# Three edits to a stack of four graph layers: ordered waits on GpSimd, a 128-row tile for the exponentials, and a PSUM tile of its own for the last block product

## The chip, the cores and the metric

The kernel runs on one core of one Trainium2 chip. The metric is the device time of one execution in microseconds (us); a figure for a kernel is the median of several executions. Engines: PE is TensorE's matmul, PEld its weight load, DVE is VectorE, ACT is ScalarE, POOL is GpSimd, SP is SyncE, which here issues all DMAs.

## What is computed

128 graphs of 128 nodes with 512 features go through four layers; each layer ends in a residual sum and a layernorm. Everything is fp32.

```python
def _L0_gnn_ref(X, A, kernel, bias):
    Ah = A + jnp.eye(A.shape[-1], dtype=A.dtype)[None, :, :]
    dh = jax.lax.rsqrt(jnp.sum(Ah, axis=-1))
    An = dh[:, :, None] * Ah * dh[:, None, :]
    return jax.nn.relu(jnp.einsum('bnm,bmf,fc->bnc', An, X, kernel) + bias)

def _L1_gnn_ref(x, adj_matrix, W_qk, W_v):
    q, k = jnp.split(jnp.einsum('bnd,ed->bne', x, W_qk), 2, axis=-1)
    v = jnp.einsum('bnd,ed->bne', x, W_v)
    scores = jnp.einsum('bnd,bmd->bnm', q, k) / ATT_DIM ** 0.5
    w = jax.nn.softmax(jnp.sum(scores * adj_matrix, axis=-1, keepdims=True), axis=1)
    return w * v

def _L2_gnn_ref(x, adj, W):
    deg = jnp.sum(adj, axis=-1, keepdims=True)
    agg = jnp.einsum('bij,bjf->bif', adj, x) / jnp.maximum(deg, EPS)
    return jax.nn.relu(jnp.einsum('bnf,of->bno', jnp.concatenate([x, agg], axis=2), W))

def _L3_gnn_ref(X, A, W, b):
    A_hat = A + jnp.eye(A.shape[-1], dtype=A.dtype)
    d = A_hat.sum(axis=-1) ** (-0.5)
    return jnp.einsum('bij,bjf->bif', A_hat * d[:, :, None] * d[:, None, :], X @ W + b)

x = _layernorm(x + _L0_gnn_ref(x, adj, L0_gnn_kernel, L0_gnn_bias), axis=-1)
x = _layernorm(x + _L1_gnn_ref(x, adj, L1_gnn_W_qk, L1_gnn_W_v), axis=-1)
x = _layernorm(x + _L2_gnn_ref(x, adj, L2_gnn_W), axis=-1)
x = _layernorm(x + _L3_gnn_ref(x, adj, L3_gnn_W, L3_gnn_b), axis=-1)
```

## The kernel before

**Tiles and loop.** Four graphs make a tile, so there are 32 tiles (t). The main loop runs one pass a tile: it does layers 0 and 1 of tile t interleaved with layers 2 and 3 of tile u = t - 1, and prepares tile t + 1. Tiles 0 and 1 are started in `begin` (here called the head), and the last tile is finished after the loop (the tail), where the graphs go in pairs.

**Names.** `ana` holds the adjacency of a tile, scaled by degrees (`d`, `dm`); `anT` and `arT` are its transposes. `agg0`, `agg2`, `agg3` are aggregated features, copied by ACT from the PSUM tiles `p_agg`; `xT1`, `xT2` are transposed x. In the loop x is transposed through DRAM (SP writes `xT2s`, reads `xT2y`, and DVE finishes in 32x32 blocks); at the head and the tail by TensorE (`p_xT`).

**Products with weights.** `project` computes each 128x512 by 512x512 product by Strassen's scheme in Winograd's form, in seven block products B11, T1, B21, B22, T2, T3, T4. `left_sums` makes the sums of the left operand on POOL (s1, s2, s4, and one in place; in the profile `agg3s`, `xT1s` and so on, and the tile's own name for the one in place). The products go to PSUM tiles `p_o` of a pool of five; DVE adds them up in the SBUF blocks `sa`, `sb`, `u2`, `u5` (`s_o`, `sb_o`, `u_o` in the profile) and into x. T2, T3 and T4 share one PSUM tile v: T3 and T4 are accumulated on what is there, so T4 may not start before DVE has read v for the block u5. T4 and what follows it are put off (`tails`) until after the first product of the next projection, except after the last one. Layer 1 does the same with tiles `p_v`.

**Layernorm.** `norm_stats`: DVE's bn_stats and bn_aggr give `mv`; POOL makes `rstd` (an add, then a power) and `mr`; ACT makes `nmr` and applies both to x. For layer 3 `norm_last` takes the sums on ACT (`row`, `square`), and POOL works on `last`.

**Softmax of layer 1.** `l1_scores` has TensorE's `p_sc` and four DVE operations `scr` that leave the row weights `w` (128x4). `l1_softmax` transposes w (`p_w`, 4x128), takes the minimum, the exponential and its sum on ACT, and scales by the reciprocal on DVE: the tile `e` of 4 rows by 128. `l1_add` transposes e back (`p_ws`, 128x4), copies it to `ws`, and adds ws * v to x by four DVE operations for each pair of graphs.

**What sets the order.** All operations are first recorded in a `Plan` with estimated durations. `schedule` is a list scheduler: it simulates the five engines, takes at each step the ready operation with the earliest latest start, and so fixes the order on every engine. It has one resource besides the engines: `port`, that any POOL operation and any DVE operation with two SBUF operands of full size hold while they run, one at a time. `emit` issues the operations in that order. On the chip each engine runs its own queue in order, and waits between engines are made from data dependences alone: the turns at the port are planned, but nothing enforces them. All operations are issued from line 271, so that the profile tells them apart by tile names.

Of the kernel before, what the change touches and what calls it, by code (L numbers as in the profile page):

```python
# [10 lines left out]
FP = mybir.dt.float32  # L11
AF = mybir.ActivationFunctionType
ALU = mybir.AluOpType
AX = mybir.AxisListType

P = 128
K = 32
Q = P // K
G = 4
# [101 lines left out]
class Op:  # L121
    def __init__(self, engine):
        self.engine, self.dur, self.lat, self.size, self.port, self.calls, self.preds, self.succs = engine, 0, 0, 0, False, [], set(), []
        self.last, self.start, self.end = float("inf"), None, None


class Plan:
# [2 lines left out]

    ENGINES = ("tensor", "vector", "scalar", "gpsimd", "sync")
    HOP = 200
    LAND, FLIGHT = 1600, 9
    HEAD, BUS = 40000, (62, 95)

    def __init__(self, nc, est):
        self.nc, self.est, self.ops, self.tags, self.group, self.dram = nc, est, [], {}, None, None
        for e in self.ENGINES:  # L140
            setattr(self, e, Recorder(self, e))

# [54 lines left out]
    def schedule(self):  # L197
        number = {op: i for i, op in enumerate(self.ops)}
        for (_, tag, bufs), tiles in self.tags.items():
            used = []  # L200
            for t in sorted((t for t in tiles if t.ops), key=lambda t: number[t.ops[0]]):
                if len(used) == bufs:
                    old = used.pop(min(range(bufs), key=lambda i: number[used[i].ops[-1]]))
                    assert number[old.ops[-1]] < number[t.ops[0]], (tag, bufs)
                    for op in t.ops:
                        if op.preds.isdisjoint(t.ops):
                            op.preds.update(old.ops)
                used.append(t)
        now = 0
        for op in self.ops:  # L210
            assert all(number[p] < number[op] for p in op.preds)
            for p in op.preds:
                p.succs.append(op)
            if op.engine == "tensor":
                op.last = now
                now += op.dur
        for op in reversed(self.ops):
            due = min([s.last - self.hop(op, s) for s in op.succs], default=now)
            op.last = min(op.last, due - op.dur)
        queue = {e: [] for e in self.ENGINES}  # L220
        waiting = {op: len(op.preds) for op in self.ops}
        free, bus, port = dict.fromkeys(self.ENGINES, 0), 0, 0
        pe = [op for op in self.ops if op.engine == "tensor"]
        for op in self.ops:
            if not op.preds:
                queue[op.engine].append((0, number[op], op))
        done, landed = [], []
        while len(done) < len(self.ops):
            best = None
            for e in self.ENGINES:  # L230
                q = queue[e]
                if e == "tensor":
                    q = [c for c in q if c[2] is pe[0]]
                if not q:
                    continue
                q = [(max(c[0], port if c[2].port else 0),) + c[1:] for c in q]
                at = max(free[e], min(c[0] for c in q))
                pick = min((c for c in q if c[0] <= at), key=lambda c: (c[2].last, c[1]))
                for c in q:
                    if at < c[0] < at + pick[2].dur and c[2].last < at + pick[2].dur and c[2].last < pick[2].last:  # L240
                        pick, at = c, c[0]
                if best is None or at < best[0]:
                    best = at, e, pick[2]
            at, e, op = best
            queue[e] = [c for c in queue[e] if c[2] is not op]
            if e == "sync" and len(landed) >= self.FLIGHT:
                at = max(at, landed[-self.FLIGHT])
            op.start, op.end = at, at + op.dur
            free[e] = op.end
            if op.port:  # L250
                port = op.end
            if e == "sync":
                bus = max(bus, op.end + self.LAND) + op.size / self.BUS[at > self.HEAD]
                op.lat = max(op.lat, bus - op.end)
                landed.append(op.end + op.lat)
            if e == "tensor":
                pe.pop(0)
            done.append(op)
            for s in op.succs:
                waiting[s] -= 1  # L260
                if not waiting[s]:
                    queue[s.engine].append((max(p.end + self.hop(p, s) for p in s.preds), number[s], s))
        return done
# [4 lines left out]
    def emit(self):  # L268
        for op in self.schedule():
            for method, args, kw in op.calls:  # L270
                getattr(getattr(self.nc, op.engine), method)(  # L271
                    *[v.real() if isinstance(v, Ref) else v for v in args],
                    **{k: v.real() if isinstance(v, Ref) else v for k, v in kw.items()})


class Recorder:
# [35 lines left out]
def kernel(  # L312
# [10 lines left out]
    b3: bass.AP,  # L323
    out: bass.AP,
):
    nc = Plan(tc.nc, estimate)
    B = x.shape[0]
    NT = B // G
    last = NT - 1
# [57 lines left out]
        nc.tensor.transpose(p[:, 0], ident, ident)  # L387
    nhalf = const.tile([P, G], FP, tag="nhalf", name="nhalf")
    nc.vector.memset(nhalf, -0.5)
    w0_sb = weight(w0, "w0_sb", nc.sync)  # L390
    b0_sb = broadcast_row(b0, "b0_sb", nc.sync)
    wqk_sb = tp.tile([P, C, 2 * ATT], FP, tag="row", name="wqk_sb", bufs=1)
# [133 lines left out]
    def project(name, t, parts, first, c11, fin, hooks=None, after=lambda: None, pairs=(0, 1), early=True):  # L526

        hooks = hooks or {}  # L530
        qs = slice(pairs[0], pairs[-1] + 1)

        def region():
            return ps_b.tile([P, 2, H], FP, tag="pb", name=f"p_{name}_{t}")[:, qs]

        def operand(left_, k):
            s = st[left_, t]
            if isinstance(s, Ref):
                return s.rearrange("p (q r) (h c) n -> p q r h c n", r=2, h=2)[:, :, 0, (B11, B21).index(k)]
            return s[k]  # L540

        def product(p, k, fresh):
            with nc.unit():
                for q in pairs:
                    for i, (left_, w) in enumerate(parts):
                        for c in range(2):
                            nc.tensor.matmul(p[:, q - pairs[0], :], operand(left_, k)[:, q, c, :], w[:, c, k, :],
                                             start=(fresh and q == pairs[0] and i == 0 and c == 0),
                                             stop=(i == len(parts) - 1 and c == 1), skip_group_check=True)
            for f in hooks.get(k, ()):  # L550
                f()

        def block(tag):
            return tp.tile([P, 2, H], FP, tag=tag, name=f"{tag}_{name}_{t}", bufs=2 if tag == "s" else 1)[:, qs]

        g, q, v = region(), None, None
        product(g, B11, True)
        sa, sb = first(g, block)
        finish_tails()
        if early:  # L560
            product(g, B21, False)
            c11(g, block)
        q = region()
        product(q, T1, True)
        u5 = block("u5")
        nc.vector.tensor_tensor(u5, q, sb, ALU.add)
        if not early:
            product(g, B21, False)
            c11(g, block)
        v = region()  # L570
        product(v, T2, True)
        u2 = block("u2")
        nc.vector.tensor_tensor(u2, v, sb, ALU.add)
        product(q, B22, False)
        nc.vector.tensor_tensor(u2, q, u2, ALU.add)
        fin(0, 1, u2)
        norm_stats(name, t, 0, pairs)
        product(v, T3, False)
        nc.vector.tensor_tensor(u5, v, u5, ALU.add)
        fin(1, 1, u5)  # L580

        def tail():
            product(v, T4, False)
            nc.vector.tensor_tensor(sa, v, sa, ALU.add)
            fin(1, 0, sa)
            norm_stats(name, t, 1, pairs)
            after()

        tails.append(tail)
# [126 lines left out]
    def l1_softmax(t):  # L716
# [1 line left out]
        nc.tensor.transpose(p[:G, :], st.pop(("w", t)), ident)  # L718
        mn = sp.tile([G, 1], FP, tag="mn", name=f"mn_{t}")
        nc.vector.tensor_reduce(mn, p[:G, :], AX.X, ALU.min)  # L720
        e = sp.tile([G, P], FP, tag="e", name=f"e_{t}", bufs=1)
        ssum = sp.tile([G, 1], FP, tag="ssum", name=f"ssum_{t}")
        nc.scalar.activation(e, p[:G, :], AF.Exp, bias=mn, scale=-1.0, accum_out=ssum)
        rsum = sp.tile([G, 1], FP, tag="rsum", name=f"rsum_{t}")
        nc.vector.reciprocal(rsum, ssum)
        nc.vector.tensor_scalar(e, e, rsum, None, ALU.mult)
        st["e", t] = e

    def l1_out(t, hooks):

# [44 lines left out]
    def l1_add(t):  # L775

        p = ps_t.tile([P, P], FP, tag="pt", name=f"p_ws_{t}")
        nc.tensor.transpose(p[:, :G], st.pop(("e", t)), ident[:G, :G])
        ws = sp.tile([P, G], FP, tag="ws", name=f"ws_{t}")
        nc.vector.tensor_copy(ws, p[:, :G])  # L780
        for r in range(2):
# [167 lines left out]
```

## Time and profile before

| what | us |
|---|---|
| median of 3 executions (lowest, highest) | 2450.66 (2450.37, 2451.76) |
| the profiled execution, its own time | 2451.53 |
| its span, first to last instruction | 2449.8 |
| PE busy, 12462 matmuls | 2437.9 |
| DVE busy, 3396 instructions | 1714.5 |
| POOL busy, 1580 instructions | 1316.0 |
| ACT busy, 2117 instructions | 996.4 |
| one pass of the loop (1073.72 to 1149.36) | 75.64 |

The granted TensorE clock is 0.999, and DMAs move 97 GB/s on average. In the profile, a busy time is a sum over instructions, whose ends are modelled for matmuls; in a dense stretch the starts are what to go by. An idle time in brackets is that of the engine just before an instruction, with what released it.

### The profile page before, as it was taken

The numbers are of one execution on the slowest core, as the hardware profiler recorded it, in microseconds if no ns is written. First come the engines' busy times: TensorE is split into PE (matmuls) and PEld (weight loads), VectorE is DVE, ScalarE is ACT, GpSimd is POOL, SyncE is SP. The second block draws the span as 40 slices with busy tenths as digits, with TensorE's granted clock in tenths as the row PEclk, the third lists the DMA queues.
The fourth block names the chain that finished last, engine by engine and source line by source line (L and its number), as shares of the span: only waits on it lengthen the run. The fifth ranks groups of instructions, "written<-read, shape, count | busy, mean of one in ns | idle before, by whom it ended". The sixth has DMA issues, their size and how long they took to land.

```text
span 2449.8 us, 35470 instructions
## 1 busy us (share of the span) xinstructions
PE 2437.9 (100%) x12462; PEld 2087.3 (85%) x12462; DVE 1714.5 (70%) x3396; ACT 996.4 (41%) x2117; POOL 1316.0 (54%) x1580
## 2 busy tenths in 40 slices
PE   9999999999999999999999999999999999999998
PEld 7888888888888888888888888888888888888887
DVE  7767766677666777766776667766677676777666
ACT  4334343443434444344443444333444334443345
POOL 6464555555555555555455554645546455555543
PEclk9999999999999999999999999999999999999999
DMA  5133233442424423244332443234442333423220
GB/s 181 48 99 104 73 108 91 125 125 57 116 78 125 125 69 109 78 121 125 84 93 82 117 125 104 73 99 104 120 125 61 96 102 117 125 74 96 67 80 35
DMA packets 393266, 241.15 MB, mean 98 GB/s; under 512 B 140416, under 2 KB 358016, under 8 KB 393088
## 3 DMA queue, kind: packets, MB, share of 16 engines
q1 hardware_dynamic: 393088, 238.88, 35.4%
q8 instruction: 99, 1.62, 0.3%
q14 instruction: 79, 0.65, 0.1%
HBM read 126.62 MB, written 112.20 MB: 97 GB/s over the span
## 4 chain that ended last, share of the span: by engine, by line
PE 96%; DMA 1%; DVE 1%; POOL 1%; SPq 0%; issue 0%; ACT 0%; POOLq 0%; DVEq 0%
PE p_o L271 61%; PE p_v L271 20%; PE p_agg L271 14%; PE p_sc L271 1%; SPq L271 0%; DMA x<-in_x_dram 0%; PE p_w L271 0%; DVE x L271 0%; DMA xT1s<-x 0%; DVE u_o L271 0%; PE p_ws L271 0%; DMA xT1y<-xT1s 0%; PE p_xT L271 0%; POOL xT2s L271 0%; DMA xT2y<-xT2s 0%
## 5 line engine op out<-in xcount | busy, mean ns | idle before, releaser
L271 PE MATMUL p_o<-w_sb,agg 128*128 128x256 f32 x2048 | 471.3, 380 | 0.9 <-DVE u_o L271 0.9
L271 PEld LDWEIGHTS p_o<-w_sb,agg 128*128 128x128 f32 x2048 | 386.1, 190 | 52.8 <-DVE u_o L271 0.9
L271 ACT COPY agg<-p_agg 128x512 f32<-128x512 f32 (+1 forms) x415 | 226.3, 553 | 406.0 <-PE p_agg L271 405.8
L271 PE MATMUL p_v<-wv_sb,xT 128*128 128x320 f32 x1024 | 291.7, 433 | 0.1
L271 PE MATMUL p_o<-w2x_sb,xT 128*128 128x256 f32 x1024 | 263.0, 379 | 1.0 <-ACT xT L271 1.0
L271 DVE TENSOR_TENSOR v<-p_v,v 128x320 f32<-128x320 f32 x316 | 154.5, 490 | 155.4 <-PE p_v L271 154.8
L271 PE MATMUL p_o<-w2a_sb,agg 128*128 128x256 f32 x1024 | 262.8, 379 | 0.0
L271 PEld LDWEIGHTS p_v<-wv_sb,xT 128*128 128x128 f32 x1024 | 191.9, 190 | 76.7 <-ACT xT L271 0.6
L271 PEld LDWEIGHTS p_agg<-anT,x 128*128 128x128 f32 x2048 | 238.7, 192 | 7.0 <-DVE anT L271 0.5
L271 DVE TENSOR_TENSOR u_o<-p_o,u_o 128x512 f32<-128x512 f32 (+1 forms) x196 | 129.1, 671 | 160.6 <-PE p_o L271 159.1
L271 PE MATMUL p_agg<-anT,x 128*128 128x128 f32 x2048 | 239.4, 275 | 0.3 <-DVE anT L271 0.3
L271 PEld LDWEIGHTS p_o<-w2x_sb,xT 128*128 128x128 f32 x1024 | 194.2, 190 | 30.8 <-ACT xT L271 1.4
L271 PE MATMUL p_v<-wv_sb,xT1s 128*128 128x320 f32 x768 | 217.6, 433 | 0.8 <-POOL xT1s L271 0.6
L271 PEld LDWEIGHTS p_o<-w2a_sb,agg 128*128 128x128 f32 x1024 | 194.6, 190 | 26.4
L271 POOL TENSOR_SCALAR rstdo<-mvo 128x2 f32<-128x2 f32 (+1 forms) x131 | 35.7, 272 | 320.9 <-DVE mvo L271 318.3
L271 PE MATMUL p_o<-w2x_sb,xT2s 128*128 128x256 f32 x768 | 197.2, 379 | 0.0
L271 PE MATMUL p_o<-w2a_sb,agg2s 128*128 128x256 f32 x768 | 197.1, 379 | 0.0
L271 ACT ACTIVATE x<-x,nmro,rstdo 128x512 f32<-128x512 f32 x256 | 195.0, 808 | 3.4
L271 PEld LDWEIGHTS p_v<-wv_sb,xT1s 128*128 128x128 f32 x768 | 145.5, 190 | 59.0 <-POOL xT1s L271 2.0
L271 PE MATMUL p_o<-w_sb,agg0s 128*128 128x256 f32 x768 | 181.1, 379 | 0.4 <-DVE u_o L271 0.4
L271 PE MATMUL p_o<-w_sb,agg3s 128*128 128x256 f32 x744 | 173.8, 383 | 0.0
L271 DVE BATCH_NORM_STATS2 bno<-x 128x6 f32<-128x512 f32 x258 | 170.4, 682 | 3.9
(146 smaller groups left out, 4255.8 us busy)
## 6 DMA issues: line engine op xcount, KB each, us to landing
x<-in_x_dram SPq DMA_DIRECT2D x31, 1024.0 KB, 6.5
out_dram<-x SPq DMA_DIRECT2D x31, 1024.0 KB, 5.4
xT2s<-x SPq DMA_DIRECT2D x120, 256.0 KB, 2.8
xT2y<-xT2s SPq DMA_DIRECT2D x240, 128.0 KB, 2.7
xT1s<-x SPq DMA_DIRECT2D x120, 256.0 KB, 2.5
xT1y<-xT1s SPq DMA_DIRECT2D x240, 128.0 KB, 3.1
sa<-ana SPq DMA_DIRECT2D x120, 128.0 KB, 3.2
ya<-sa SPq DMA_DIRECT2D x120, 128.0 KB, 3.3
```

Of the source, the lines that this page charges most:

```text
L271: getattr(getattr(self.nc, op.engine), method)(*[v.real() if isinstance(v, Ref) else v for v in args], **{k: v.real() if isinstance(v, Ref ...
```

## The change

It has three parts.

- In `schedule`, when an operation takes the port, the plan now also remembers the one that had it before (`owner`). If the new one is on POOL, the former is on DVE, and the POOL operation was otherwise ready less than 500 ns (`CLOSE`) after the port came free, the POOL operation is given a wait on that DVE operation (`op.after`), which `emit` adds. The planned order itself is made as before.
- The exponentials are kept in one constant tile `e_sb` of 128x128, zeroed once at the start; the softmax works on its first 4 rows, as before on the tile e. The transpose back takes the whole tile with the whole identity, so that p_ws is 128x128, of which the first 4 columns are read.
- In the very last projection, DVE adds v to sa before the product T4, T4 goes to a PSUM tile of its own, and sa then takes that.

```diff
@@ class Plan
-    HOP = 200
+    HOP, CLOSE = 200, 500
...
-    def __init__(self, nc, est):
-        self.nc, self.est, self.ops, self.tags, self.group, self.dram = nc, est, [], {}, None, None
+    def __init__(self, tc, est):
+        self.tc, self.nc, self.est, self.ops, self.tags, self.group, self.dram = tc, tc.nc, est, [], {}, None, None
@@ schedule
-        free, bus, port = dict.fromkeys(self.ENGINES, 0), 0, 0
+        free, bus, port, owner = dict.fromkeys(self.ENGINES, 0), 0, 0, None
...
             if op.port:
-                port = op.end
+                ready = max((p.end + self.hop(p, op) for p in op.preds), default=0)
+                if e == "gpsimd" and owner is not None and owner.engine == "vector" and ready < port + self.CLOSE:
+                    op.after = owner
+                port, owner = op.end, op
@@ emit
-                getattr(getattr(self.nc, op.engine), method)(
+                op.ins = getattr(getattr(self.nc, op.engine), method)(
                     *[v.real() if isinstance(v, Ref) else v for v in args],
-                    **{k: v.real() if isinstance(v, Ref) else v for k, v in kw.items()})
+                    **{k: v.real() if isinstance(v, Ref) else v for k, v in kw.items()}).ins
+            if op.after is not None:
+                self.tc.add_manual_dep(op.ins, op.after.ins.name, mybir.DependencyInfo(
+                    mybir.DependencyClass.Sync, mybir.DependencyReason.DATA))
@@ tile_gnn_stack_kernel
+    e_sb = const.tile([P, P], FP, tag="e_sb", name="e_sb")
+    nc.vector.memset(e_sb, 0.0)
@@ project
         def tail():
-            product(v, T4, False)
-            nc.vector.tensor_tensor(sa, v, sa, ALU.add)
+            p = v
+            if (name, t, pairs[-1]) == ("o3", last, 1):
+                nc.vector.tensor_tensor(sa, v, sa, ALU.add)
+                p = region()
+            product(p, T4, p is not v)
+            nc.vector.tensor_tensor(sa, p, sa, ALU.add)
@@ l1_softmax
-        e = sp.tile([G, P], FP, tag="e", name=f"e_{t}", bufs=1)
+        e = e_sb[:G, :]
@@ l1_add
-        nc.tensor.transpose(p[:, :G], st.pop(("e", t)), ident[:G, :G])
+        nc.tensor.transpose(p, e_sb, ident)
```

More of the change, by code (lines that the diff above doesn't have):

```diff
@@ L123, in __init__ @@
         self.engine, self.dur, self.lat, self.size, self.port, self.calls, self.preds, self.succs = engine, 0, 0, 0, False, [], set(), []
-        self.last, self.start, self.end = float("inf"), None, None
+        self.last, self.start, self.end, self.after = float("inf"), None, None, None
 class Plan:
     ENGINES = ("tensor", "vector", "scalar", "gpsimd", "sync")
-    HOP = 200
+    HOP, CLOSE = 200, 500
     LAND, FLIGHT = 1600, 9
     HEAD, BUS = 40000, (62, 95)
-    def __init__(self, nc, est):
-        self.nc, self.est, self.ops, self.tags, self.group, self.dram = nc, est, [], {}, None, None
+    def __init__(self, tc, est):
+        self.tc, self.nc, self.est, self.ops, self.tags, self.group, self.dram = tc, tc.nc, est, [], {}, None, None
         for e in self.ENGINES:
@@ L325 @@
 ):
-    nc = Plan(tc.nc, estimate)
+    nc = Plan(tc, estimate)
     B = x.shape[0]
@@ L726, in l1_softmax @@
         nc.vector.tensor_scalar(e, e, rsum, None, ALU.mult)
-        st["e", t] = e
     def l1_out(t, hooks):
```

## The prediction

> **What bounds the kernel now.** I read the page first, then the waits, then the timeline of one loop pass, of the head and of the tail.
>
> ```profile
> PE 2437.9 (100%) x12462; PEld 2087.3 (85%) x12462; DVE 1714.5 (70%) x3396; ACT 996.4 (41%) x2117; POOL 1316.0 (54%) x1580
> ...
> PE 96%; DMA 1%; DVE 1%; POOL 1%; SPq 0%; issue 0%; ACT 0%; POOLq 0%; DVEq 0%
> ```
>
> TensorE (PE) is the chain and is called busy throughout, so only time inside that "busy" or at the ends can be won. The view of waits shows where weight loads (PEld) came late:
>
> ```profile
> PEld p_ws L271 <- issue: 10.7, 32, 0.4
> PEld p_w L271 <- issue: 9.6, 27, 0.4
> ```
>
> Both are the single small transposes of the softmax, 32 each. The timeline of one pass (start, us):
>
> ```profile
> 1023.57 1.28 POOL L271 TENSOR_TENSOR agg3s<-agg 128x512 f32<-128x512 f32 x1 [8.85 <-ACT agg L271]
> 1023.64 1.76 DVE L271 TENSOR_TENSOR ana<-ana,ident 128x512 f32<-128x512 f32 x1
> 1024.44 1.94 PE L271 MATMUL p_o<-w_sb,agg 128*128 128x256 f32 x8
> 1025.32 0.27 DVE L271 SCALAR_TENSOR_TENSOR scr<-p_sc,dmn,v 128x64 f32<-128x64 f32 x1
> 1026.36 0.27 PE L271 MATMUL p_w<-ident,w 128*4 128x128 f32 x1
> 1026.47 1.89 PE L271 MATMUL p_o<-w_sb,agg3s 128*128 128x256 f32 x8
> 1028.20 1.89 PE L271 MATMUL p_o<-w_sb,agg 128*128 128x256 f32 x8
> 1030.02 0.22 PE L271 MATMUL p_ws<-ident,e 4*128 4x4 f32 x1
> ...
> 1030.17 3.72 PE L271 MATMUL p_o<-w_sb,agg3s 128*128 128x256 f32 x16
> 1033.73 7.07 PE L271 MATMUL p_o<-w_sb,agg 128*128 128x256 f32 x32
> ```
>
> Starts count here, since ends are modelled. Eight p_o take 1.73 (1026.47 to 1028.20). The next eight take 1.82 up to p_ws (0.09 lost), p_ws takes 0.15, and the sixteen behind it 3.56 instead of 3.46 (0.10 lost): one p_ws costs 0.09 + 0.15 + 0.10 = 0.34, in the finer starts 0.348. The same sum holds for all 32 of them, although e was ready between 0.39 and 5.06 us earlier: the loss is not a wait for data.
>
> p_w is different. From 1024.44 to 1026.36 are 1.92; in the pass at 2310.38, where w was ready 0.68 early, the same stretch is 1.78. So 0.145 is lost, in 28 of the 32 passes. There w is late (last scr to p_w 0.155 in each) because scr starts at 1025.32 instead of about 1024.64 (p_sc ends 1024.44, and PE to DVE takes 0.2 in this trace): the ana operation before it took 1.76, beside POOL's agg3s, against 0.68 for the same operation undisturbed (1047.28).
>
> **What the Trainium skill says.** "TensorEngine Tiling (Array Packing)", Key Properties: "Mode switching requires drain". With "TensorE: Matmul & The Clock Gate", step by step: a weight load is pulled ahead of running matmuls if the row groups don't conflict or it goes to the background buffer. The trace agrees for p_ws (4 rows): its load starts at 1030.02 with its own matmul, not before. For 128x128 transposes it finds no loss: eight p_xT from 86.84 to 87.71, 0.109 each, and four p_o behind them at once in 0.87. "SBUF — State Buffer", Who interferes with whom: a DVE instruction with two SBUF inputs and a GpSimd instruction that reads SBUF share a port; whichever is second blocks. The 1.76 against 0.68 agrees.
>
> **The change part by part.** My sum is made against the profiled execution, 2451.53 us (span 2449.8 and 1.7 around it); the median is 2450.66, 0.87 lower.
>
> *Exponentials in 128 rows.* p_ws becomes one 128x128 transpose. I take the 0.109 of p_xT: 0.348 - 0.109 = 0.24 saved, in 31 passes 7.4 us. In the last pass nothing: the PE stall at 2392.00 is set by DVE's chain from p_ws, so an earlier PE waits there longer (0.04 left). Bounds: all of it, 7.7; or none, should the drain belong to the lone transpose rather than its 4 rows. The exponential, reciprocal and multiplication still touch 4 rows. The zeroing at the start lies in DVE's idle time before 3.58. One p_agg a pass gains a wait on a p_ws some 12 us older: nothing.
>
> *GpSimd waits.* The instruction orders are the old ones but for the tail; 347 POOL instructions are given a wait on the DVE operation planned before them. In the trace 287 of these started before that DVE operation ended, so most waits bind. In the loop the first gain is p_w: agg3s has to wait for ana (14 passes ana,ident, 14 ana,d). ana then ends near 1024.33, scr starts on PE's 1024.64, w is ready 0.68 earlier and the 0.145 goes: 28 x 0.145 = 4.1 us. Next late is nothing: in the 2 passes with w early, PE runs on. What stands behind the wait: agg3s starts at about 1024.41 rather than 1023.57, 0.84 later; its result had 1.62 to spare before PE. The other waits of a pass: rstdv on the last x<-v (1.47 later, twice a pass about 1.5 to 1.7) delays nmrv on ACT and the x for PE's p_agg, which had 2.9 or more, and the first transposed-sum xT2s had 1.7 (median). agg3 (T3), up to 3.0 later, had 4.2, and agg2, 2.4 later, 12.5. I cost these at nothing; above, the price is what exceeds the spare.
>
> *Head, to 50 us.* Gain: sb_o (14.58) now follows agg0s, DVE's agg0s are not blocked (2.90 for two before, about 0.8 free), u_o is there at 19 instead of 20.30, and the stall at 20.36 goes: 0.52 + 0.10. Loss: agg0s2 of tile 1 (28.07) waits for DVE's two wv_sb (about 30.5), agg0s4 and agg0 follow x operations, so rstdo behind them runs near 37.1 instead of 34.77, and mro at 38.2 instead of 36.31. ACT's normalisation and copies take 2.4 up to the first p_xT: PE gets it at 40.8 instead of 39.62. Part is recovered, since ACT idled 0.57 and POOL's xT1s was held by rstdo: PE's xT1s product at 47.7 instead of 47.10. Net +0.6; bounds -1.3 (the stalls at 20.36 and from 40.57 to 47.10 are 2.6 in all; half of them gone) and +1.7.
>
> *Tail.*
>
> ```profile
> 2391.77 1.66 DVE L271 SCALAR_TENSOR_TENSOR x<-v,ws,x 128x256 f32<-128x256 f32 x4
> ...
> 2392.46 0.24 POOL L271 TENSOR_TENSOR mrv<-mvv,rstdv 128x2 f32<-128x2 f32 x1
> 2392.73 0.20 ACT L271 ACTIVATE nmrv<-mrv 128x2 f32<-128x2 f32 x1 [7.52 <-POOL mrv L271]
> ...
> 2393.83 2.05 PE L271 MATMUL p_agg<-arT,x 128*128 128x128 f32 x16
> ...
> 2397.43 1.13 PE L271 MATMUL p_o<-w2x_sb,xT 128*128 128x256 f32 x4 [0.68 <-ACT xT L271]
> ```
>
> Here mrv gets a wait on the fourth x<-v, which ends 2393.43: mrv near 2393.5, 1.04 late, and x, p_agg with it, since x was on time by 0.05 alone. At 2397.43 ACT's queue gives 0.4 back (nmrv of the second half no longer holds it). Net +0.65; bounds 0 and +1.1.
>
> *Last block product.*
>
> ```profile
> 2440.41 1.03 PE L271 MATMUL p_o<-w_sb,agg 128*128 128x256 f32 x4
> 2441.47 0.42 DVE L271 TENSOR_TENSOR u_o<-p_o,u_o 128x256 f32<-128x256 f32 x1 [0.44 <-PE p_o L271]
> ...
> 2441.95 1.13 PE L271 MATMUL p_o<-w_sb,agg 128*128 128x256 f32 x4 [0.52 <-DVE u_o L271]
> ...
> 2446.26 0.55 DVE L271 TENSOR_SCALAR x<-x,mvo,rstdo 128x512 f32<-128x512 f32 x1
> ```
>
> T4 in its own PSUM starts at 2441.27 (2440.41 + 4 x 0.216), 0.68 earlier. DVE has one more add (0.42) and becomes the bound: x<-u_o moves into its idle 0.44 before 2441.47, then u_o, the new add, x, the last add at about 2442.5 (before 2443.12), x, two bn_stats, mvo at 2444.25 instead of 2444.57. POOL's order brings rstdo's power straight behind its sum, no longer behind the power of last: end 0.6 earlier. Bounds 0.3 and 0.9.
>
> Sum: -7.4 - 4.1 + 0.6 + 0.65 - 0.6 = -10.9, 2440.6 for an execution like the profiled one, 0.87 less against the median: 2439.7.
>
> **Rivals.** (A) p_w keeps its loss: ana stays slow or scr is held by something else. For: DVE runs other two-input operations there. Against: the two early passes. 2439.7 + 4.1 = 2443.8. (B) The drain stays with p_ws: 2439.7 + 7.4 = 2447.1. For: p_w is a lone transpose with a late load too. Against: p_w with early w (67.10, 98.97) loses nothing. (C) The waits cost 2 to 4 us more in head, tail or some passes: 2442 to 2444. For: queues of POOL and ACT are in order, and the wait's own latency is not in my sums. (D) Slower: the transposed-sum path of a pass. rstdv's wait (1.69 + 0.08) delays x, SP's DMA xT2s (1044.38) behind it, xT2y, the DVE transposes and POOL's xT2s, with 1.72 spare before PE. Reaching PE whole and losing a 0.93 slot of SP's queue, it stalls 2.70 - 1.72 = 0.98 a pass, 29 times 28: 2468. It decides from 2.1 on (1.72 + 10.9/29). Against: nmrv stood behind ACT's row until 1041.90 anyway, so only 0.8 of 1.77 passes.
>
> **How the numbers follow.** Forecast 0.64, A 0.10, B 0.07, C 0.13, D 0.06. The range runs from 2437.2 (head at its good bound) to 2445.5 (C and A in); B and D are outside. 0.2%, 4.9 us, is what a measurement of this kernel can tell from no change: faster is below 2445.8 (forecast, A, C: 0.87), same 0.07 (B), slower 0.06 (D).
>
> **What would show it.** p_ws in a stretch of p_o: 0.11 and no longer load behind it; p_w's lateness gone and ana at 0.68 beside no agg3s; the pass shortened from 75.64 to about 75.25; p_xT near 40.8; p_agg near 1.0 late at the tail. A pass above 75.5, or PE waits in the loop for xT2s, agg3s or x, would prove it wrong.

## The result and the profile after

The changed kernel takes 2439.84 us (median of 5 executions, 2439.40 to 2440.78) where the kernel before takes 2450.66: ratio 0.9953, 95% interval 0.9943 to 0.9964. Its profiled execution took 2440.58 with a span of 2438.8, against 2451.53 and 2449.8 before: 11.0 less span.

The page of the changed kernel, first the busy times, then the chain by engine:

```profile
PE 2425.6 (99%) x12462; PEld 2088.6 (86%) x12462; DVE 1676.0 (69%) x3398; ACT 999.5 (41%) x2117; POOL 1230.8 (50%) x1580
...
PE 95%; DMA 1%; DVE 1%; POOL 1%; SPq 1%; ACT 1%; issue 0%; POOLq 0%; DVEq 0%; ACTq 0%
```

DVE's busy time fell by 38.5 us and POOL's by 85.2, with two DVE instructions more than before. The runs below tell the parts apart: with the added waits alone (e2) the two are busy for 1671.0 and 1233.1, with the 128 rows alone (e1) for 1713.2 and 1317.1. So it is the waits, and part of what had been called busy was one engine held up by the other. Of TensorE's 11.0 only about 4 came from there, and about 7 from the rows of p_ws; the rest of that busy time had not been on its path.

In the view of waits of the weight loads, p_ws and p_w led with 10.7 and 9.6 us. Now the longest are these (us in all, times, longest), and neither p_ws nor p_w is among them:

```profile
PEld p_xT L275 <- ACT xT1y L275: 2.7, 3, 2.0
PEld p_agg L275 <- ACT x L275: 1.3, 1, 1.3
...
PEld p_v L275 <- POOL xT1s L275: 1.3, 2, 0.7
```

The timeline of the pass that the prediction showed (start and duration in us, engine, operation):

```profile
1019.32 0.68 DVE L275 TENSOR_TENSOR ana<-ana,ident 128x512 f32<-128x512 f32 x1
...
1020.12 1.95 PE L275 MATMUL p_o<-w_sb,agg 128*128 128x256 f32 x8
1020.15 1.27 POOL L275 TENSOR_TENSOR agg3s<-agg 128x512 f32<-128x512 f32 x1 [8.30 <-ACT agg L275]
1020.32 0.28 DVE L275 SCALAR_TENSOR_TENSOR scr<-p_sc,dmn,v 128x64 f32<-128x64 f32 x1 [0.31 <-PE p_sc L275]
...
1021.90 0.27 PE L275 MATMUL p_w<-ident,w 128*4 128x128 f32 x1
...
1022.01 1.89 PE L275 MATMUL p_o<-w_sb,agg3s 128*128 128x256 f32 x8
...
1023.74 1.89 PE L275 MATMUL p_o<-w_sb,agg 128*128 128x256 f32 x8
...
1025.25 0.14 PEld L275 LDWEIGHTS p_ws<-ident,e_sb 128*128 128x128 f32 x1
...
1025.46 0.27 PE L275 MATMUL p_ws<-ident,e_sb 128*128 128x128 f32 x1
...
1025.57 3.62 PE L275 MATMUL p_o<-w_sb,agg3s 128*128 128x256 f32 x16
```

ana is done in 0.68 before agg3s starts; scr waits for PE's p_sc and no longer for ana; from 1020.12 to p_w are 1.78, where there were 1.92. Around p_ws nothing is lost: 1.72 for the eight p_o before it (1023.74 to 1025.46), 0.11 for p_ws, whose load now starts 0.21 ahead of it.

The tail, and the end:

```profile
2381.07 1.66 DVE L275 SCALAR_TENSOR_TENSOR x<-v,ws,x 128x256 f32<-128x256 f32 x4
...
2382.87 0.20 POOL L275 TENSOR_TENSOR mrv<-mvv,rstdv 128x2 f32<-128x2 f32 x1 [1.19 <-DVE x L275]
...
2384.20 2.05 PE L275 MATMUL p_agg<-arT,x 128*128 128x128 f32 x16 [0.94 <-ACT x L275]
...
2430.41 1.89 PE L275 MATMUL p_o<-w_sb,agg 128*128 128x256 f32 x8
...
2434.42 0.22 POOL L275 TENSOR_SCALAR rstdo<-mvo 128x1 f32<-128x1 f32 x1
2434.73 0.62 POOL L275 TENSOR_TENSOR rstdo<-rstdo,nhalf 128x1 f32<-128x1 f32 x1
...
2435.38 0.55 DVE L275 TENSOR_SCALAR x<-x,mvo,rstdo 128x512 f32<-128x512 f32 x1 [0.46 <-POOL rstdo L275]
```

mrv now waits 1.19 for the fourth x<-v, and p_agg pays for it. At the end the last eight p_o run as one row, without the 0.68 between the fours.

### The profile page after: what moved, and what is told of

It is laid out like the page before. It is cut to its first block, busy times and chain, and to the rows that moved or that the text cites. A ratio compares the mean times of both kernels' runs of the same rounds, so it can differ in the third digit from the quotient of the medians.

```text
span 2438.8 us, 35587 instructions
## 1 busy us (share of the span) xinstructions
PE 2425.6 (99%) x12462; PEld 2088.6 (86%) x12462; DVE 1676.0 (69%) x3398; ACT 999.5 (41%) x2117; POOL 1230.8 (50%) x1580
## 3 DMA queue, kind: packets, MB, share of 16 engines
q8 instruction: 99, 1.62, 0.3%
## 4 chain that ended last, share of the span: by engine, by line
PE 95%; DMA 1%; DVE 1%; POOL 1%; SPq 1%; ACT 1%; issue 0%; POOLq 0%; DVEq 0%; ACTq 0%
PE p_o L275 60%; PE p_v L275 20%; PE p_agg L275 14%; PE p_sc L275 1%; SPq L275 1%; DMA xT1s<-x 0%; DMA xT1y<-xT1s 0%; POOL xT2s L275 0%; ACT x L275 0%; DMA xT2y<-xT2s 0%; DVE x L275 0%; DVE xT L275 0%; PE p_xT L275 0%; POOL rstdo L275 0%; DVE ana L275 0%
## 5 line engine op out<-in xcount | busy, mean ns | idle before, releaser
L275 ACT ACTIVATE nmro<-mro 128x2 f32<-128x2 f32 (+1 forms) x130 | 26.5, 204 | 368.0 <-POOL mro L275 367.9
```

The costliest lines, as they stand in the source:

```text
L275: op.ins = getattr(getattr(self.nc, op.engine), method)(*[v.real() if isinstance(v, Ref) else v for v in args], **{k: v.real() if isinstan ...
```

## The experiments

All times are medians beside runs of the kernel before on the same chip, whose median there was 2451.86 (e1 to e4), 2451.62 (e5, e6, e7, e9) and 2451.63 (e8, e10 to e12), about 1 us above that of the result. So differences are compared, not times. Where a difference is small, the trace says more than the median. This table is worked out from start times of PE's rows in one trace of each kernel (us, spans to the hundredth, 2449.75 for the kernel before): the head from the first p_agg of tile 0 to the first p_w; the pass as the mean of two passes (p_w of tile 7 to that of tile 9); the passes from the p_w of tile 2 to that of tile 31; the tail from there to the end of the span.

| kernel | head | pass | passes | tail |
|---|---|---|---|---|
| before | 58.79 | 75.633 | 2190.24 | 65.67 |
| after | 59.01 | 75.257 | 2179.93 | 65.38 |
| after, again (e12) | 59.01 | 75.257 | 2179.21 | 65.37 |
| 128 rows alone (e1) | 59.05 | 75.401 | 2183.25 | 65.64 |
| waits alone (e2) | 58.94 | 75.493 | 2185.95 | 66.63 |
| PSUM alone (e3) | 59.31 | 75.632 | 2190.43 | 64.86 |
| 28 waits (e4) | 58.24 | 75.256 | 2180.80 | 64.83 |
| 28 waits, again (e11) | 58.24 | 75.257 | 2178.87 | 64.83 |
| all but the 28 (e5) | 59.00 | 75.401 | 2183.35 | 65.37 |
| 28 and one of the head (e10) | 58.75 | 75.257 | 2179.53 | 64.83 |

### One part at a time

The kernel before with only the tile e_sb and its transpose:

```diff
-        e = sp.tile([G, P], FP, tag="e", name=f"e_{t}", bufs=1)
+        e = e_sb[:G, :]
...
-        nc.tensor.transpose(p[:, :G], st.pop(("e", t)), ident[:G, :G])
+        nc.tensor.transpose(p, e_sb, ident)
```

> The kernel before with only the exponentials in a tile of 128 rows, so that p_ws is one 128x128 transpose. Theory (the 4 rows of p_ws make the array drain): each p_ws then takes 0.11 up to the next matmul, nothing is lost before or behind it, 0.24 is saved in 31 passes, 7.5 us in all: 2443.2. p_w keeps its wait of 0.145. Rival (the loss belongs to a lone transpose, whatever its rows): 2450.7. A second question is the two waits of PE for the transposed-sum product at tile 10 and tile 26, which grew by 0.19 and 0.32 with the whole change: if they grow because PE arrives earlier, they grow here as well; if the added waits make the operands late, they stay at 0.29 and 0.05.

Measured: 2444.88, ratio 0.9971 (0.9959 to 0.9983), 7.0 less. A pass is 0.232 shorter, p_ws takes 0.109 up to the next matmul and 0 is lost before it, and p_w keeps its lateness in 28 passes. The rival falls. On the second question neither reading held: in this execution PE's waits at tile 10 and 26 were gone.

The kernel before with only `op.after` in the plan (the first part of the change's diff):

> The kernel before with only the waits of GpSimd. Theory: -4.1 in the passes (p_w's wait gone), +0.6 head, +0.65 tail: 2447.8. If these waits also make the operands at tile 10 and 26 late, 0.5 more: 2448.3. Rival (p_w late for another reason): nothing won, head and tail lost: 2451.9. Rival (the waits cost in the passes too): above 2449.

Measured: 2448.81, ratio 0.9988 (0.9981 to 0.9995), 3.05 less. A pass is 0.140 shorter and p_w is late nowhere; p_ws still loses its 0.094 before and 0.104 behind. The tail is 0.96 longer: 0.64 of it comes with the late mrv at its start, and 0.3 near its end, where PE waits for the last agg31s; the whole change, whose plan orders this end differently, has no such wait. Both rivals fall.

The kernel before with only the new `tail()`:

> The kernel before with only the last block product in PSUM of its own. Theory: the stall of 0.68 before the last four p_o goes, and PE and DVE end 0.6 earlier: 2450.1, the difference being below what the medians can tell, but not below what the profile of the last 10 us can. Rival (DVE has one more add and is the chain of the end, so that nothing comes of it): p_o starts earlier but the last x and the end do not: 2450.7.

Measured: 2450.87, ratio 0.9996 (0.9988 to 1.0005): not told from no change, as expected. Its trace: the 0.68 before the last p_o is gone, and from the start of the last stretch of p_o<-agg31s (2438.32, before 2437.82) to the end of the span are 11.20 instead of 11.93, and the whole tail is 0.81 shorter, so 0.7 to 0.8 is won and not 0.6. The rival falls.

The three differences, 7.0, 3.05 and 1.0, add up to 11.0, the whole change's 10.8 within what the medians can tell. In the passes the parts don't overlap: 0.232 and 0.140 make 0.372, and the whole change's pass is 0.376 shorter. In the tail they don't simply add (-0.03, +0.96 and -0.81 against -0.29 for the whole), most of the difference being e2's wait for the last agg31s.

### Which of the 347 waits matter

The changed kernel with a wait only where the first agg3s of a pass follows ana (28 waits); `named` gives the name of an operation's output:

```diff
-            if op.after is not None:
+            if op.after is not None and (named(op), named(op.after)) == ("agg3s1", "ana"):
```

> The changed kernel with 28 of its 347 waits: only the first sum of the third layer's aggregates (agg3s, the first of a pass) on the DVE multiplication of the adjacency (ana). Theory (this collision alone made w late): p_w waits for nothing in 28 passes, and head and tail are as before: 2450.7 - 7.5 - 4.1 - 0.6 = 2438.5, about 1.3 below the whole change. Rival (other waits are needed for w, or for order in the passes): p_w keeps 0.145 in some or all passes: 2440 to 2442.6.

Measured: 2439.69, ratio 0.9950 (0.9935 to 0.9964), 12.2 less than before. p_w waits nowhere. The pass is 75.256, the same as with all 347.

The opposite, with `!=` in that line, so that 319 waits stay:

> The changed kernel without those 28 waits of agg3s on ana; its other 319 waits stay. Theory (only these keep ana clear of agg3s): ana takes 1.76 again in these passes and p_w waits 0.145 in 28 of them: 4.1 more than the whole change, 2443.9 where before is 2450.7 (6.7 below before). Rival (the other waits shift GpSimd so far that ana is clear of it anyway, or one wait in an earlier place orders both): p_w waits for nothing, 2439.8 (10.8 below before).

Measured: 2444.17, ratio 0.9970 (0.9957 to 0.9982), 7.45 less than before. p_w is late in 28 passes again and the pass is 75.401, that of e1 to the nanosecond: in the passes the 319 other waits win nothing that PE feels. The timeline of its pass shows the collision again:

```profile
1020.61 1.29 POOL L280 TENSOR_TENSOR agg3s<-agg 128x512 f32<-128x512 f32 x1 [7.46 <-ACT agg L280]
...
1020.69 1.76 DVE L280 TENSOR_TENSOR ana<-ana,ident 128x512 f32<-128x512 f32 x1
...
1022.37 0.27 DVE L280 SCALAR_TENSOR_TENSOR scr<-p_sc,dmn,v 128x64 f32<-128x64 f32 x1
...
1023.41 0.27 PE L280 MATMUL p_w<-ident,w 128*4 128x128 f32 x1
```

agg3s starts 0.08 ahead of ana, and ana ends 0.55 after it. Together e4 and e5 show that for p_w these 28 waits are enough, and needed.

### What makes the small transpose dear

Four forms of p_ws in the changed kernel. The first two are ordinary matmuls of two passes, which differ only in their rows; the plan is told the transpose's duration so that the order stays.

```diff
-        nc.tensor.transpose(p, e_sb, ident)
+        nc.tensor.matmul(p[:, :G], e_sb[:G, :], ident[:G, :G], start=True, stop=True)
```

> The changed kernel with p_ws as an ordinary matmul of the 4 rows of e with a 4x4 identity (two passes, not the transpose's one), as a control for the next run. Theory (4 rows make the array drain before and behind it): in a stretch of p_o about 0.09 lost before its first pass and 0.10 behind its last, as before, with its own time on top.

```diff
+        nc.tensor.matmul(p[:, :G], e_sb, ident[:, :G], start=True, stop=True)
```

> The same matmul with all 128 rows of e and 128x4 of the identity: the same two passes, the same 4 moving columns, only the rows differ from the run before. Theory (rows): nothing lost before it and behind it; p_ws up to the next p_o takes two weight loads of 128 columns at most, about 0.2. Rival (the 4 moving columns make it slow, since too little runs while the next weights load): the same loss as with 4 rows, 0.1 behind it.

```diff
+        nc.tensor.transpose(p[:, :32], e_sb[:32, :], ident[:32, :32])
```

> The changed kernel with p_ws as a transpose of 32 rows with a 32x32 identity. Theory (any tile that doesn't use all rows drains): 0.09 lost before and 0.10 behind it, as with 4 rows. Rival (only a tile of under 32 rows[...] drains): 0.11 and nothing lost, as with 128.

```diff
+        nc.tensor.transpose(p[:, :64], e_sb[:64, :], ident[:64, :64])
```

> The changed kernel with p_ws as a transpose of 64 rows with a 64x64 identity, after 32 rows drained as 4 do. Theory (every tile with fewer rows than the 128 of its neighbours drains): 0.09 lost before it and 0.1 behind it, about 0.37 in all. Rival (half the array is enough to let the load go ahead): 0.11, nothing lost.

One execution each, on two chips, so that the single times alone can't rank the forms. From the last p_o before p_ws to the third behind it, less three undisturbed p_o of 0.216, median of 30 passes:

| rows x moving columns | us | lost before p_ws | single time of the kernel |
|---|---|---|---|
| 4 x 4, transpose (before) | 0.347 | 0.094 | |
| 128 x 128, transpose (after) | 0.111 | 0 | 2440.58 |
| 4 x 4, two passes (e6) | 0.507 | 0.093 | 2452.72 |
| 128 x 4, two passes (e7) | 0.223 | 0 | 2442.97 |
| 32 x 32, transpose (e9) | 0.374 | 0.094 | 2449.02 |
| 64 x 64, transpose (e8) | 0.399 | 0.094 | 2449.34 |

The timeline of one pass of e9 and of e7:

```profile
1027.06 1.89 PE L275 MATMUL p_o<-w_sb,agg 128*128 128x256 f32 x8
1028.88 0.14 PEld L275 LDWEIGHTS p_ws<-ident,e_sb 32*128 32x128 f32 x1 [0.33 <-issue]
1028.88 0.25 PE L275 MATMUL p_ws<-ident,e_sb 32*128 32x32 f32 x1
1029.06 3.72 PE L275 MATMUL p_o<-w_sb,agg3s 128*128 128x256 f32 x16
```

```profile
1024.60 1.89 PE L275 MATMUL p_o<-w_sb,agg 128*128 128x256 f32 x8
1026.11 0.41 PEld L275 LDWEIGHTS p_ws<-ident,e_sb 128*128 128x128 f32 x2
1026.33 0.28 PE L275 MATMUL p_ws<-ident,e_sb 128*128 128x4 f32 x2
1026.47 3.70 PE L275 MATMUL p_o<-w_sb,agg3s 128*128 128x256 f32 x16
```

With 32 rows the eight p_o take 1.82, and the load starts with its own matmul after 0.33 of waiting for nothing that the profile shows. With 128 rows they take 1.73 and the load starts 0.22 ahead, though only 4 columns move. So the loss before p_ws goes with the rows, and half the array is no better than 4 rows: the rivals for e9 and e8, by which 32 or 64 rows pass freely, fall. The rival for e7 is right in part: 4 moving columns lose nothing before, but 0.083 behind, where the second p_o comes 0.299 after the first instead of 0.216. As ordinary matmuls, 128 rows are 0.28 a pass cheaper than 4: 0.09 of it before p_ws, 0.17 from p_ws to the next p_o (0.31 and 0.14), and only 0.02 behind. So that the loss behind p_ws goes with the rows is not shown: with few moving columns most of it stays. That the numbers sit in a constant tile now is not what helps, since e8 and e9 use the same tile.

### Whether the other waits pay, and noise

The changed kernel with the 28 waits and the one at the head that puts sb_o behind DVE's agg0s; the 28 alone again; and the changed kernel as it is:

```diff
-            if op.after is not None:
+            if op.after is not None and (named(op), named(op.after)) in (("agg3s1", "ana"), ("sb", "agg0s4")):
```

> The changed kernel with 29 waits: the 28 of agg3s on ana, and the one of the head that keeps GpSimd's first bias sum off DVE's agg0s. Theory (the other 318 waits win nothing, and those of head and tail cost: at the head p_xT 1.2 later, at the tail p_agg 1.1 later, of which 0.3 and 0.6 reach PE's end): about 1.3 below the whole change, and the stall of 0.5 to 1.0 near 20.4 us gone. Rival (the waits that are left out keep other collisions away that PE does feel): within 0.3 of the whole change or above it.

> The kernel with the 28 waits alone, again, beside the whole change on the same chip. Theory: 0.8 to 1.3 below the whole change, the stall near 20.4 us at the head being there or not from execution to execution. Rival: no difference to the whole change that the intervals can tell.

> The changed kernel unaltered, on the same chip as the two before, as their control: 10.8 below the kernel before.

Measured, five executions each: e10 2439.02 (2438.71 to 2439.25), ratio 0.9948 (0.9935 to 0.9960); e11 2439.48 (2438.89 to 2439.87), ratio 0.9950 (0.9936 to 0.9964); e12 2439.78 (2439.45 to 2439.99), ratio 0.9951 (0.9938 to 0.9963), 11.85 below before. e10 lies 0.76 below the whole change, and no execution of one reaches the other's; at 12.6 below the kernel before it is the furthest of all kernels here, though executions of e11 overlap with it. e11's 0.3 can't be told: that e4 came out about 1.3 further below its kernel before than the whole change had, on another chip, is not confirmed side by side. Both gains are below the expected 1.3 and 0.8: in the tail 0.54 came (65.37 to 64.83), at the head of e10 0.26. There the stall near 20.4 went, but 0.39 appeared before p_o at 35.75.

**Why the head differs between executions of one program.** The timeline of the head of the kernel before, and of the changed one:

```profile
8.72 0.69 DVE L271 TENSOR_REDUCE deg<-ana 128x4 f32<-128x512 f32 x1 [0.47 <-DMA ana<-in_adj_dram]
...
12.33 1.41 DVE L271 TENSOR_TENSOR w_sb<-w_sb 128x512 f32<-128x512 f32 x2
...
19.03 0.67 DVE L271 TENSOR_TENSOR u_o<-p_o,b_sb 128x512 f32<-128x512 f32 x1
```

```profile
9.49 0.69 DVE L275 TENSOR_REDUCE deg<-ana 128x4 f32<-128x512 f32 x1 [1.12 <-DMA ana<-in_adj_dram]
...
13.31 1.41 DVE L275 TENSOR_TENSOR w_sb<-w_sb 128x512 f32<-128x512 f32 x2
...
17.86 0.68 DVE L275 TENSOR_TENSOR u_o<-p_o,b_sb 128x512 f32<-128x512 f32 x1
```

DVE waits for the adjacency of tile 1: 0.47 in before, 0.72 in e1, 0.98 in e3, not at all in e4 and e11. PE's stall near 20.4 was 0.52, 0.77 and 0.97 in the first three and 0.06 at most in the other two: it is that late DMA, handed through. From w_sb to u_o DVE needs 6.70 without waits at the head (before, e3, e4) and 4.55 with them (after, e5): they take 2.15 of blocking out, so that u_o is early and the stall gone although the DMA was 1.12 late. In e10, where sb_o's is the only wait at the head, it is 4.54: that one wait does it.

**Waits in the passes that come and go.** PE's waits for the transposed sum are not the change's either. At tile 10, e4 and e11, which are the same kernel, in two executions:

```profile
774.12 1.30 DVE L280 STREAM_TRANSPOSE xT<-xT1y 128x512 f32<-128x512 f32 x2 [4.13 <-DMA xT1y<-xT1s]
775.57 1.27 POOL L280 TENSOR_TENSOR xT1s<-xT 128x512 f32<-128x512 f32 x1 [4.20 <-DVE xT L280]
776.89 1.10 PEld L280 LDWEIGHTS p_v<-wv_sb,xT1s 128*128 128x128 f32 x5 [1.34 <-POOL xT1s L280]
```

```profile
772.69 1.30 DVE L280 STREAM_TRANSPOSE xT<-xT1y 128x512 f32<-128x512 f32 x2 [2.37 <-DMA xT1y<-xT1s]
774.14 1.27 POOL L280 TENSOR_TENSOR xT1s<-xT 128x512 f32<-128x512 f32 x1 [2.45 <-DVE xT L280]
```

In e4 DVE waits 4.13 for the DMA xT1y and PE stands 1.10 (with 0.63 at tile 26); in e11 DVE waits 2.37 and PE at neither place. That is the whole difference between their passes, 2180.80 and 2178.87, with 0.1 behind each stall. These waits vary between executions of one kernel by more than the 0.5 by which they grew from before to after, so that 0.5 is no effect of the change that these runs could show. Such waits come mostly at these two tiles, though not only: e9 has one of PE for xT1s at 1308.70 and e6 one at 2218.42. What makes the DMA late there stays open; it was not tried.

## Why the prediction was right

The forecast was the case that came: 2440.6 for an execution like the profiled one, and it took 2440.58; 2439.7 for the median, and it is 2439.84. By its own steps:

- **128 rows.** Predicted 7.4, measured 0.236 in 31 passes, 7.3. In the last pass nothing was won, as said: p_ws is 0.24 cheaper, and the stall behind it grew by 0.20. The premise, that the rows make it dear, was argued from one row of the profile; e7 against e6 shows it, but for the loss behind.
- **p_w.** Predicted 4.1, measured 4.2 in the same 28 passes. Its cause, the collision of ana with agg3s, is shown by e4 and e5.
- **What stood behind the waits was costed at nothing.** That held in every pass, but the cover shrank. From the end of the operand to PE's use of it (medians over the passes), agg3s had 1.62 and has 0.59, the x for p_agg 3.12 and 1.84, and agg3 (T3), in the 14 passes in which it waits for ana, 4.18 and 2.24. For agg3s the prediction had allowed 0.84; 1.03 went. Rival D's spare was misread: the 1.7 for the transposed-sum xT2s was the median of two groups, about 1.0 in every other pass and 1.7 in those between, before and after. Taken pass by pass, the spare shrank by a median of 0.06, and by 0.7 to 0.8 in three passes. So D fell not because 1.7 was enough, but because little of the delay reached xT2s; with 1.0 to spare in half the passes it had stood nearer than the prediction held.
- **Head.** Predicted +0.6 (40.8 for p_xT, 47.7 for the xT1s product), measured 40.85 and 47.54, and +0.33 at the first p_w, of which 0.12 is a later first p_agg. The single steps came as said, but one was mis-sized and the sum has no one value: DVE was freed of 2.15 where the prediction took 0.8, and the stall that this removed was as long as a DMA happened to be late. Heads without these waits took 58.24 to 59.31, with all of them 58.94 to 59.01: the waits take a late DMA's cost away and add their own.
- **Tail.** Predicted +0.65 from +1.04 and -0.4, measured +1.08 and -0.44 (e2 against before). Without the wait on mrv (e4, e10, e11) it goes.
- **Last block product.** Predicted -0.6, with 0.9 as the far bound; measured, from the start of the last p_o<-agg31s to the end, -0.95, and -0.73 alone (e3). The term was too small: both of the prediction's effects came one behind the other. Set against the same start, mvo is 0.45 earlier, where 0.32 was predicted, and the power of rstdo, no longer behind that of last, another 0.4. The remaining 0.1 is a shorter way from the last x to the end of the span.
- **Not in the sum:** the +0.5 of the two DMA waits above. It hid the 0.35 by which the last product, and the 0.3 by which the head, came out better than the sum had them, and single executions of the changed kernel lie between 2439.40 and 2440.78. So the closeness of the total is in part luck; the two large terms are not.
- **The range.** Its low end, 2437.2, was given as the head at its good bound; that alone makes 2439.7 - 1.9 = 2437.8.

"TensorEngine Tiling (Array Packing)", Key Properties, was cited for a drain at a change of tiling mode. The runs fit it, with 0.09 lost before p_ws and 0.10 behind it for 4, 32 and 64 rows among 128; that a drain is what takes this time no run here shows. The blocking that "SBUF — State Buffer", Who interferes with whom, describes is what e5 shows beside the changed kernel: ana at 1.76 and at 0.68.

## What to carry to other kernels

A matmul that fills only some rows can cost more than its size in a stream of full ones, as p_ws did (0.347 against 0.111); where the other rows can be zero at no cost, try a full tile. When two engines share a port, don't order all their work: find the one collision whose late end PE waits for, and order that one, since waits elsewhere take spare time from operands, and cost 0.5 at the tail here. Starts of TensorE's rows, compared between two stretches of the same work, find losses of 0.1 us that busy shares hide.

## What the runs showed of the hardware

- A transpose of 32 or of 64 rows among matmuls of 128 rows cost 0.374 and 0.399 us, more than one of 4 rows (0.347), and one of 128 rows 0.111.
- Two passes of 128 rows with 4 moving columns lost nothing before and 0.083 behind; the transpose p_w with its 4-column weights but 128 moving columns loses nothing on either side.
- Loads differ between executions of the same work by more than the parts of this change are worth: the adjacency of tile 1 made DVE wait for 0 to 1.5 us at the head, and the two stalls at tile 10 and 26 came to between 0 and 1.7 us for one kernel.
